# The last 16 steps of a chunked recurrence: PSUM tiles for each batch, a repeated product, and a copy placed one unit later

## The chip, the cores and the metric

The kernel runs on one core of a Trainium2 chip. The metric is the device time of one execution in microseconds (us). The program is one launch, and everything is in float32. A core has TensorE (PE, matrix products into PSUM), VectorE (DVE), ScalarE (ACT), GpSimd (POOL) and SyncE (SP), each with its own queue, and a set of DMA engines that move data between HBM and SBUF.

## The reference, cut to what matters

The input is x of shape 4 x 128 x 64 x 64: four images ("batches"), 128 channels, 4096 positions each. Layer 0 is an attention over the positions of the group-normed input, added to x. Layer 1 is a causal attention over the same 4096 positions as tokens, added, and then a recurrent block, also added:

```python
Wx = einsum('bti,hi->bth', layernorm(t), W)
Wx = (Wx - mean) * rsqrt(var + eps) * gamma + beta      # mean, var over all tokens
def step(yt, wx_t):
    yt = sigmoid(wx_t + yt @ V.T)
    return yt, yt
_, ys = scan(step, zeros, Wx over time)
t = t + ys
```

The recurrence runs along the 4096 tokens of each batch, and each step needs the step before it.

## The kernel before, in words

**The attention part** takes nearly all of the time. Its work is cut into units (`units`), in each of which a pair of key blocks of 128 is scored against a tile of up to 512 queries (`score`), exponentiated by ScalarE and multiplied with the values (`product`). Side work (normalisation, projections, the recurrence's input) is written as Python generators that are advanced one `yield` per unit by `step`. `ffn` (L745 on) makes the recurrence's input of one tile: it normalises a tile of the layer-1 output, multiplies it with W and lets ScalarE copy the product into the buffer `WX` (L772). The last query tile of the last batch is cut into two parts of 384 and 128 queries (`LAST` = 384), so that only the small part is left when the attention ends.

**The recurrence** follows. A batch's 4096 tokens are cut into chunks, of 16 tokens for batches 0 and 1 (256 chunks) and of 32 for batches 2 and 3 (128 chunks), and all chunks of a batch advance side by side as columns of one product. A chunk begins with 12 warm-up steps (`WARM`) over the last 12 tokens of the chunk before it, from a state of 0.5; a check at the end (`ok`, L1114 on) compares the state after the warm-up with the state that the chunk before it ended with, and a general kernel would run if they differed. So batches 0 and 1 have 12 + 16 = 28 steps, and batches 2 and 3 have 12 + 32 = 44. `last` is 28.

There are three chains of steps (`chains`): batch 0, batch 1, and batches 2 and 3 together. For a chain, `seed` (L1045) lets VectorE write gain times WX of two steps into a PSUM tile of one bank, `advance` (L1064, L1065) lets TensorE add FV times the state y to one step's part of the tile, and then ScalarE apply the sigmoid and write the new state into the buffer where WX of that token was. The tag of a chain (`y0`, `y1`, `y2`) has two PSUM tiles in turn. In steps 0 to 27 the three chains stand in for each other: while one waits for its sigmoid, the others compute.

From step 28 on only batches 2 and 3 are left. `advance` then splits the chain into its two batches (the list `parts`), as two products and two sigmoids in each step; both write to and read from the same PSUM tile. After each of these steps the kernel issues one product of zeros with 512 columns into a spare tile (`idle(rest, 1)`, recorded at L566, the line of the helper).

VectorE also adds the states to the residual as they get ready (`residual`, L1069), eight or four tokens of a batch at a time; the list `late` holds the additions of batches 1, 2 and 3, and a loop hands out at most one per step from step 28 on. When a batch is complete, `store` (L1074) issues two transfers of 1 MB each: batches 0 and 1 from SP's queue, batches 2 and 3 one half from SP's and one from ScalarE's queue. After the last additions VectorE works out the check (L1114 to L1123), TensorE sums it over the partitions (L1125), VectorE writes the result (L1126, L1127), and all engines load it (L1135) and branch (L1136) over the general kernel to the end of the program.

**The order of the instructions** on each engine is made when the program is built, by a scheduler that goes by the order in the source, by what depends on what and by its own estimate of when operands are ready. It also sets the semaphore waits. Where two engines touch the same PSUM tile, it orders them by the tile's bank and not by the columns that each touches. TensorE, VectorE and ScalarE each take their instructions in the order so made.

Of the kernel before, what the change touches and what calls it, by code (L numbers as in the profile page):

```python
# [25 lines left out]
F32 = mybir.dt.float32  # L26
AF = mybir.ActivationFunctionType
ALU = mybir.AluOpType
# [3 lines left out]
P = 128  # L32
QT = 512
# [432 lines left out]
WARM = 12  # L466
# [8 lines left out]
def fast_kernel(  # L475
# [9 lines left out]
    nc = tc.nc  # L485
# [4 lines left out]
    NC = [N // ch for ch in CHUNK]  # L490
# [23 lines left out]
    def load(src, shape, name):  # L514
        t = const.tile(shape, F32, name=name)
        nc.scalar.dma_start(out=t, in_=src)
        return t
# [12 lines left out]
    FV = load(fv, [P, C], "FV")  # L530
# [24 lines left out]
    WX = [wxpool.tile([P, CHUNK[b] // 2, NC[b], 2], F32, name=f"WX{b}") for b in range(2)]  # L555
    WXp = wxpool.tile([P, 2, CHUNK[2] // 2, NC[2], 2], F32, name="WXp")
# [6 lines left out]
    def idle(ps, n):  # L563

        for _ in range(n):
            nc.tensor.matmul(ps, lhsT=nil, rhs=nil.unsqueeze(1).to_broadcast([P, QT // P, P]), start=True, stop=True)  # L566
# [6 lines left out]
    with ExitStack() as actx:  # L573
# [10 lines left out]
        def misc(name):  # L584
            return ps_m.tile([P, QT], F32, tag="m", name=name)
# [107 lines left out]
        def deviations(src, eps, name):  # L693

            n = src.shape[-1] // P
            pt = misc(f"pt_{name}")
            for j in range(n):
                nc.tensor.transpose(pt[:, ts(j, P)], src[:, ts(j, P)], ident)  # L698
            stats = small.tile([P, 4, 6], F32, tag="lst", name=f"lst_{name}")
            mv = small.tile([P, 4, 2], F32, tag="lmv", name=f"lmv_{name}")  # L700
            for j in range(n):
                nc.vector.bn_stats(stats[:, j, :], pt[:, ts(j, P)])
            for j in range(n):
                nc.vector.bn_aggr(mv[:, j, :], stats[:, j, :])
            rstd = small.tile([P, 4], F32, tag="rstd", name=f"rstd_{name}")
            rsqrt(rstd[:, :n], mv[:, :n, 1], eps, n)
            return pt, mv, rstd[:, :n]

        def spread(r, name):

            n = r.shape[-1]
            g = small.tile([P, 4, 4], F32, tag="g", name=f"g_{name}")
            for q in range(4):
                nc.vector.tensor_copy(g[0:32, :n, q], r[ds(32 * q, 32), :])
            for q in range(1, 4):
                nc.vector.tensor_copy(g[ds(32 * q, 32), :n, :], g[0:32, :n, :])
            rb = tmp.tile([P, QT], F32, tag="r", name=f"rb_{name}", bufs=2)[:, : n * P]
            nc.vector.transpose(
                rb.rearrange("p (k j) -> p k j", j=32),
                g[:, :n, :].rearrange("p j q -> p (j q)").unsqueeze(2).to_broadcast([P, 4 * n, 32]),  # L720
            )
            return rb
# [23 lines left out]
        def ffn(b, c, off, w):  # L746
            name = f"f_{b}_{c}_{off}"
            cols = ds(c * QT + off, w)
            src = X2[b][:, cols]
            if b < len(kept):  # L750
                nc.sync.dma_start(out=kept[b][:, cols], in_=src)
            yield
            _, _, rstd = deviations(src, 1e-5, name)
            yield
            pw = misc(f"pw_{name}")[:, :w]
            if off == 0:
                wt[b, c] = tmp.tile([P, QT], F32, tag="w", name=f"w_{name}")
            part = wt[b, c][:, ds(off, w)]
            if w == QT - LAST:
                nc.tensor.matmul(pw, lhsT=FWc, rhs=src, start=True, stop=True)  # L760
                raw = tmp.tile([P, QT], F32, tag="a", name=f"raw_{name}")[:, :w]
                nc.scalar.copy(raw, pw)
                prow = misc(f"prow_{name}")
                idle(prow, 7)
                nc.tensor.matmul(prow[:, :w], lhsT=rstd.to_broadcast([P, P]), rhs=ident, start=True, stop=True)
                nc.vector.tensor_tensor(part, raw, prow[:, :w], ALU.mult)
                idle(misc(f"idle_{name}"), 5)
            else:
                rb = spread(rstd, name)
                nc.tensor.matmul(pw, lhsT=FWc, rhs=src, start=True, stop=True)  # L770
                nc.vector.tensor_tensor(part, pw, rb, ALU.mult)
            nc.scalar.copy(  # L772
                WX[b][:, :, ds((c * QT + off) // CHUNK[b], w // CHUNK[b]), :].rearrange("p l s t -> p s l t"),
                part.rearrange("p (s l t) -> p s l t", l=CHUNK[b] // 2, t=2),
            )
            if off + w == QT:
                nc.vector.bn_stats(stats_f[:, b * NQ + c, :], wt.pop((b, c)))
            yield
# [59 lines left out]
        for b in range(B):  # L838
            for layer in range(2):
                for c in range(NQ):  # L840
                    parts = [(0, LAST), (LAST, QT - LAST)] if (b, layer, c) == (B - 1, 1, NQ - 1) else [(0, QT)]
                    for off, w in parts:
                        n = (c * QT + off + w) // P if layer else NB
# [160 lines left out]
    with ExitStack() as fctx:  # L1004
        xback = fctx.enter_context(tc.tile_pool(name="xback", bufs=1))
        small = fctx.enter_context(tc.tile_pool(name="fsmall", bufs=1))
        ps_y = fctx.enter_context(tc.tile_pool(name="ps_y", bufs=2, space=PSUM))
# [8 lines left out]
        gain = small.tile([P, 1], F32, name="fgain")  # L1016
        rsqrt(gain, mv[:, 1:2], 1e-5, 1)
        nc.vector.tensor_tensor(gain, gain, Fgamma, ALU.mult)
        bias = small.tile([P, 1], F32, name="fbias")
# [8 lines left out]
        firstp = small.tile([P, 2, NC[2]], F32, name="firstp")  # L1028
        first = [small.tile([P, NC[b]], F32, name=f"first{b}") for b in range(2)] + [firstp[:, 0], firstp[:, 1]]
        for t in (first[0], first[1], firstp):  # L1030
            nc.gpsimd.memset(t, 0.5)
        steps = [list(range(ch - WARM, ch)) + list(range(ch)) for ch in CHUNK]
        where = {}

        def seed(g, k):

            b, m = chains[g][0], len(chains[g])
            if 2 * k >= len(steps[b]):
                return
            ps = where[g, k] = ps_y.tile([P, 2, m, NC[b]], F32, tag=f"y{g}", name=f"py{g}_{k}")  # L1040
            if k < 2:
                idle(ps.rearrange("p t h s -> p (t h s)"), 1)
            l, lo = steps[b][2 * k] // 2, int(2 * k < WARM)
            src = WXp[:, :, l] if m > 1 else WX[b][:, l].unsqueeze(1)
            nc.vector.tensor_scalar(  # L1045
                ps[:, :, :, lo:].rearrange("p t h s -> p h t s"),
                src[:, :, : NC[b] - lo, :].rearrange("p h s t -> p h t s"), gain, None, ALU.mult,
            )

        def advance(g, n):  # L1050
            b, m = chains[g][0], len(chains[g])
            if n >= len(steps[b]):
                return
            lo = int(n < WARM)
            l = steps[b][n]

            parts = [slice(h, h + 1) for h in range(2)] if n >= last else [slice(0, m)]
            for hs in parts:
                s0 = firstp[:, hs] if m > 1 else first[b].unsqueeze(1)
                wx = WXp[:, hs] if m > 1 else WX[b].unsqueeze(1)  # L1060
                dst = s0[:, :, 1:] if lo else wx[:, :, l // 2, :, l % 2]
                y = dst if lo else s0 if n == WARM else wx[:, :, (l - 1) // 2, :, (l - 1) % 2]
                ps = where[g, n // 2][:, n % 2, hs, lo:]
                nc.tensor.matmul(ps, lhsT=FV, rhs=y, start=False, stop=True, skip_group_check=True)  # L1064
                nc.scalar.activation(dst, ps, AF.Sigmoid, bias=bias)  # L1065

        def residual(b, l, n):
            xj = X[b].rearrange("p (s l t) -> p l s t", l=CHUNK[b] // 2, t=2)[:, l // 2 : (l + n) // 2]
# [2 lines left out]
        def store(b):  # L1071
            for h in range(2):
                eng = nc.scalar if h and b > 1 else nc.sync
                eng.dma_start(out=out[b, :, ts(h, N // 2)], in_=X[b][:, ts(h, N // 2)])  # L1074
# [4 lines left out]
        last = len(steps[0])  # L1079
        rest = ps_y.tile([P, QT], F32, tag="rest", name="rest", bufs=1)  # L1080
# [1 line left out]
        late += [(b, l, 8) for l in range(0, CHUNK[2] - 8, 8) for b in (2, 3)]  # L1082
        late += [(b, l, 4) for l in (CHUNK[2] - 8, CHUNK[2] - 4) for b in (2, 3)]
        for n in range(len(steps[2])):
            for g in range(3):
                advance(g, n)
            if n >= last:
                idle(rest, 1)
            if n == WARM - 1:
                for t in (first[0][:, 0:1], first[1][:, 0:1], firstp[:, :, 0:1]):  # L1090
                    nc.vector.memset(t, 0.0)
            if n % 2:
                for g in range(3):
                    seed(g, n // 2 + 2)
            if WARM < n < last and (n + 1) % 4 == 0:
                residual(0, n - WARM - 3, 4)
                if n == last - 1:
                    store(0)
            elif n >= last and late and WARM + late[0][1] + late[0][2] <= n:
                b, l, k = late.pop(0)  # L1100
                residual(b, l, k)
                if b == 1 and l + k == CHUNK[1]:
                    store(1)
# [73 lines left out]
```

## Time and profile before

| What | Value |
|---|---|
| Median of 3 runs | 2572.41 us (2571.79 to 2572.5) |
| The profiled execution: its time | 2572.15 us |
| The profiled execution: its span | 2570.4 us |
| First product of the recurrence starts | 2485.3 us |
| First product of step 28 starts | 2524.23 us |
| Last sigmoid ends | 2555.22 us |
| Last residual addition ends | 2555.93 us |
| Last stores issued (SP and ScalarE queues) | 2555.96 and 2555.97 us |
| The check's result written | 2559.91 us |
| Busy over the span: PE, DVE, ACT, POOL | 98%, 69%, 44%, 8% |
| Granted TensorE clock, mean | 0.991 |

The span is counted from the first to the last record of the profile; the execution's own time is 1.75 us longer. Times inside the execution are given from the span's start. The share of busy time is an average over stages that have different limits: the attention fills TensorE, and the last stage does not. In a line of the chain view the columns are the start in us, the length in us, and the engine, the tile written and the line; x2 is the number of records merged. One float32 product is recorded as two MATMULs.

### The profile page before, as it was taken

The page shows a single profiled execution, that of the slowest core. Times are in us where ns is not written, and L with a number is a line of the kernel's source. Part 1 is how long each engine was busy: PE and PEld are TensorE (multiplying, and loading weights), DVE is VectorE, ACT ScalarE, POOL GpSimd, SP SyncE. Part 2 cuts the span into 40 slices and gives each one's busy share as a digit, 9 for nine tenths or more (in the row PEclk, how much of TensorE's full clock was granted, in tenths as well). Part 3 has the DMA queues.
Part 4 walks back from the last instruction along what each step waited for, and adds up shares of the span by engine and source line. Part 5 has one row for each costly group of instructions (what it writes and reads, how often), then busy time and mean ns, then how long its engine had stood idle before and what let it go on. Part 6 is the DMA issues. An engine that isn't in the chain of part 4 may idle for free.

```text
span 2570.4 us, 22293 instructions
## 1 busy us (share of the span) xinstructions
PE 2514.2 (98%) x7596; PEld 1370.0 (53%) x7596; DVE 1771.7 (69%) x3534; ACT 1140.2 (44%) x1432; POOL 194.5 (8%) x281
## 2 busy tenths in 40 slices
PE   7999999999999999999999999999999999999996
PEld 4555554444555555444555555444455555544574
DVE  6776667557867677666777676765687666776565
ACT  4444434444444444444444444444444444444464
POOL 2010001101000100110100010111000000000000
PEclk9999999999999999999999999999999999999997
DMA  2000000000100000000100000000010000000013
GB/s 73 1 0 1 0 1 13 9 5 5 37 1 1 1 0 5 13 4 9 37 1 0 1 0 1 13 9 4 5 38 0 1 1 0 1 0 1 1 66 132
DMA packets 11946, 31.33 MB, mean 12 GB/s; under 512 B 2096, under 2 KB 2864, under 8 KB 10032
## 3 DMA queue, kind: packets, MB, share of 16 engines
q1 hardware_dynamic: 9216, 26.22, 2.8%
q10 hardware_dynamic: 2608, 3.61, 0.4%
q8 instruction: 61, 1.00, 0.2%
q14 instruction: 61, 0.50, 0.1%
HBM read 15.14 MB, written 14.68 MB: 12 GB/s over the span
## 4 chain that ended last, share of the span: by engine, by line
PE 90%; DVE 7%; issue 1%; ACT 1%; POOL 1%; DMA 0%; SPq 0%; POOLq 0%; DVEq 0%; ACTq 0%
PE av L966 48%; PE ps L928 17%; PE ps L921 16%; PE py L1064 2%; DVE total L963 2%; PE po L829 1%; PE pv L675 1%; PE pq L740 1%; PE pw_f L770 1%; PE pk L659 1%; PE pt L698 1%; PE pt_f L698 0%; ACT s L930 0%; POOL rstd_f L571 0%; ACT WXp L1065 0%
## 5 line engine op out<-in xcount | busy, mean ns | idle before, releaser
L963 DVE TENSOR_TENSOR total<-total,s 128x1024 f32<-128x1024 f32 (+5 forms) x810 | 881.7, 1091 | 563.1 <-ACT s L930 325.2
L966 PE MATMUL av<-s,WXp 128*128 128x512 f32 x2048 | 964.1, 593 | 0.9 <-ACT s L930 0.9
L930 ACT ACTIVATE s<-ps,shift 128x1024 f32<-128x1024 f32 x512 | 569.3, 1113 | 758.1 <-PE ps L928 737.1
L928 PE MATMUL ps<-q,K 128*128 128x512 f32 x2048 | 758.0, 492 | 2.6 <-DVE q L689 1.4
L934 ACT ACTIVATE s<-ps,zero,R 128x512 f32<-128x512 f32 (+3 forms) x607 | 404.5, 717 | 462.6 <-PE ps L921 461.1
L966 PEld LDWEIGHTS av<-s,WXp 128*128 128x128 f32 x2048 | 382.4, 189 | 299.3 <-issue 257.4
L928 PEld LDWEIGHTS ps<-q,K 128*128 128x128 f32 x2048 | 385.7, 189 | 291.6 <-issue 235.0
L966 PE MATMUL av<-s,V 128*128 128x512 f32 (+3 forms) x1214 | 505.0, 538 | 2.0 <-ACT s L934 1.7
L921 PE MATMUL ps<-q,X 128*128 128x512 f32 (+3 forms) x1214 | 503.5, 537 | 0.0
L921 PEld LDWEIGHTS ps<-q,X 128*128 128x128 f32 x1214 | 224.9, 190 | 236.3 <-issue 219.5
L966 PEld LDWEIGHTS av<-s,V 128*128 128x128 f32 x1214 | 222.0, 190 | 224.5 <-issue 195.6
L571 POOL TENSOR_TENSOR rstd<-rstd,mhalf 128x4 f32<-128x4 f32 x32 | 32.7, 1021 | 964.4 <-DVE rstd L570 964.4
L656 POOL TENSOR_SCALAR X<-X,B0v 128x512 f32<-128x512 f32 x32 | 67.5, 2112 | 250.6 <-DVE xg L654 249.1
L937 POOL TENSOR_SCALAR_AFFINE_SELECT s<-s 128x128 f32<-128x128 f32 x128 | 46.2, 366 | 519.6 <-ACT s L934 519.2
L731 DVE TENSOR_SCALAR V<-pt,lmv,rstd 128x128 f32<-128x128 f32 x128 | 43.7, 403 | 35.7 <-POOL rstd L571 35.7
L571 POOL TENSOR_TENSOR rstd_f<-rstd_f,mhalf 128x4 f32<-128x4 f32 (+2 forms) x33 | 35.8, 1085 | 408.6 <-DVE rstd_f L570 408.6
L689 DVE TENSOR_TENSOR q<-QR,qh 64x512 fp32r<-64x512 f32 x64 | 43.9, 685 | 6.3 <-PE ps L928 5.5
L671 ACT CAST K<-kh 64x512 fp32r<-64x512 f32 x32 | 19.7, 617 | 62.3 <-DVE kh L669 62.2
L797 DVE TENSOR_TENSOR t<-total 128x512 f32<-128x512 f32 x64 | 44.1, 689 | 4.4 <-PE pfw L615 2.5
L799 DVE STREAM_TRANSPOSE tt<-t 128x512 f32<-128x512 f32 x64 | 45.3, 708 | 1.9
L814 DVE SCALAR_TENSOR_TENSOR o<-rb,av 128x512 f32<-128x512 f32 x64 | 43.6, 681 | 4.1
L812 DVE STREAM_TRANSPOSE rb<-z 128x512 f32<-128x512 f32 x64 | 45.0, 703 | 1.1
(152 smaller groups left out, 1322.2 us busy)
## 6 DMA issues: line engine op xcount, KB each, us to landing
X<-in_x SPq DMA_DIRECT2D x28, 256.0 KB, 5.1
kept<-X SPq DMA_DIRECT2D x24, 256.0 KB, 2.0
Y<-kept SPq DMA_DIRECT2D x6, 1024.0 KB, 7.8
out<-Y SPq DMA_DIRECT2D x5, 1024.0 KB, 6.0
X<-in_x ACTq DMA_DIRECT2D x4, 256.0 KB, 5.4
out<-Y ACTq DMA_DIRECT2D x1, 1024.0 KB, 6.8
out<-X SPq DMA_DIRECT2D x1, 1024.0 KB, 9.7
out<-X ACTq DMA_DIRECT2D x1, 1024.0 KB, 12.6
```

The lines of the kernel that those rows point to most:

```text
L571: nc.gpsimd.tensor_tensor(dst, dst, mhalf[:, :n], ALU.pow)
L656: nc.gpsimd.tensor_scalar(xt, xt, B0v, None, ALU.add)
L799: nc.vector.transpose(tt, t)
L812: nc.vector.transpose(rb, z[:, :k].unsqueeze(2).to_broadcast([P, k, 32]))
L921: nc.tensor.matmul(ps[:, h, first[h] : w], lhsT=lhsT, rhs=q[:, off + first[h] : off + w], start=True, stop=True,)
L928: nc.tensor.matmul(ps[:, h, :], lhsT=lhsT, rhs=q[:, k, :], start=k == 0, stop=k == 1)
L930: nc.scalar.activation(s, ps, AF.Exp, bias=shift)
L934: nc.scalar.activation(part, ps[:, h, first[h] : w], AF.Exp, scale=scale, bias=zero)
L937: nc.gpsimd.affine_select(out=edge, in_=edge, pattern=[[1, P]], base=0, channel_multiplier=-1, compare_op=ALU.is_ge, fill=0.0,)
L963: nc.vector.tensor_tensor(t, t, s[:, h, f:w], ALU.add)
L966: nc.tensor.matmul(av[:, first[h] : w], lhsT=V[:, 2 * u + h, :], rhs=s[:, h, first[h] : w], start=u == 0 and h == 0, stop=2 * u + h == n - 1,)
L1064: nc.tensor.matmul(ps, lhsT=FV, rhs=y, start=False, stop=True, skip_group_check=True)
```

## The change

Three edits are made.

- In `ffn`, for the two parts of the last tile, one more `yield` stands ahead of ScalarE's copy into WX, so the copy is written one unit later in the source.
- From step 28 on, `advance_alone` takes the place of the split in `advance`. Each of batches 2 and 3 has its own PSUM tiles, made by `seed_alone`: a tile holds four steps of one batch (one bank), under the tags `y0` and `y1` that batches 0 and 1 no longer need, two tiles each in turn. The seeds for steps 28 to 31 and 32 to 35 are written at steps 25 and 27, those for 36 to 39 and 40 to 43 at steps 31 and 35.
- After each of these steps `advance_alone` issues the product of batch 3 once more (128 columns, the same state y, into the spare tile `rest`, where nobody reads it), and the product of zeros is gone.

```diff
--- before.py
+++ after.py
@@ -769,6 +769,8 @@
                 rb = spread(rstd, name)
                 nc.tensor.matmul(pw, lhsT=FWc, rhs=src, start=True, stop=True)
                 nc.vector.tensor_tensor(part, pw, rb, ALU.mult)
+            if w < QT:
+                yield
             nc.scalar.copy(
                 WX[b][:, :, ds((c * QT + off) // CHUNK[b], w // CHUNK[b]), :].rearrange("p l s t -> p s l t"),
                 part.rearrange("p (s l t) -> p s l t", l=CHUNK[b] // 2, t=2),
@@ -1035,8 +1037,6 @@
         def seed(g, k):
 
             b, m = chains[g][0], len(chains[g])
-            if 2 * k >= len(steps[b]):
-                return
             ps = where[g, k] = ps_y.tile([P, 2, m, NC[b]], F32, tag=f"y{g}", name=f"py{g}_{k}")
             if k < 2:
                 idle(ps.rearrange("p t h s -> p (t h s)"), 1)
@@ -1047,22 +1047,37 @@
                 src[:, :, : NC[b] - lo, :].rearrange("p h s t -> p h t s"), gain, None, ALU.mult,
             )
 
+        def seed_alone(h, k):
+
+            ps = where["alone", h, k] = ps_y.tile([P, 4, NC[2]], F32, tag=f"y{h}", name=f"pz{h}_{k}")
+            l = steps[2][4 * k] // 2
+            nc.vector.tensor_scalar(
+                ps.rearrange("p (l t) s -> p l t s", t=2),
+                WXp[:, h, l : l + 2].rearrange("p l s t -> p l t s"), gain, None, ALU.mult,
+            )
+
+        def move(ps, y, dst):
+            nc.tensor.matmul(ps, lhsT=FV, rhs=y, start=False, stop=True, skip_group_check=True)
+            nc.scalar.activation(dst, ps, AF.Sigmoid, bias=bias)
+
         def advance(g, n):
             b, m = chains[g][0], len(chains[g])
-            if n >= len(steps[b]):
-                return
             lo = int(n < WARM)
             l = steps[b][n]
-
-            parts = [slice(h, h + 1) for h in range(2)] if n >= last else [slice(0, m)]
-            for hs in parts:
-                s0 = firstp[:, hs] if m > 1 else first[b].unsqueeze(1)
-                wx = WXp[:, hs] if m > 1 else WX[b].unsqueeze(1)
-                dst = s0[:, :, 1:] if lo else wx[:, :, l // 2, :, l % 2]
-                y = dst if lo else s0 if n == WARM else wx[:, :, (l - 1) // 2, :, (l - 1) % 2]
-                ps = where[g, n // 2][:, n % 2, hs, lo:]
-                nc.tensor.matmul(ps, lhsT=FV, rhs=y, start=False, stop=True, skip_group_check=True)
-                nc.scalar.activation(dst, ps, AF.Sigmoid, bias=bias)
+            s0 = firstp if m > 1 else first[b].unsqueeze(1)
+            wx = WXp if m > 1 else WX[b].unsqueeze(1)
+            dst = s0[:, :, 1:] if lo else wx[:, :, l // 2, :, l % 2]
+            y = dst if lo else s0 if n == WARM else wx[:, :, (l - 1) // 2, :, (l - 1) % 2]
+            move(where[g, n // 2][:, n % 2, :, lo:], y, dst)
+
+        def advance_alone(n):
+
+            l = steps[2][n]
+            for h in range(2):
+                y = WXp[:, h, (l - 1) // 2, :, (l - 1) % 2]
+                move(where["alone", h, n // 4][:, n % 4], y, WXp[:, h, l // 2, :, l % 2])
+
+            nc.tensor.matmul(rest[:, : NC[2]], lhsT=FV, rhs=y, start=True, stop=True)
 
         def residual(b, l, n):
             xj = X[b].rearrange("p (s l t) -> p l s t", l=CHUNK[b] // 2, t=2)[:, l // 2 : (l + n) // 2]
@@ -1082,16 +1097,20 @@
         late += [(b, l, 8) for l in range(0, CHUNK[2] - 8, 8) for b in (2, 3)]
         late += [(b, l, 4) for l in (CHUNK[2] - 8, CHUNK[2] - 4) for b in (2, 3)]
         for n in range(len(steps[2])):
-            for g in range(3):
-                advance(g, n)
-            if n >= last:
-                idle(rest, 1)
+            if n < last:
+                for g in range(3):
+                    advance(g, n)
+            else:
+                advance_alone(n)
             if n == WARM - 1:
                 for t in (first[0][:, 0:1], first[1][:, 0:1], firstp[:, :, 0:1]):
                     nc.vector.memset(t, 0.0)
-            if n % 2:
+            if n % 2 and n + 3 < last:
                 for g in range(3):
                     seed(g, n // 2 + 2)
+            elif n in (last - 3, last - 1) or n >= last and n % 4 == 3 and n + 5 < len(steps[2]):
+                for h in range(2):
+                    seed_alone(h, (last // 4 if n == last - 3 else (n + 1) // 4 + 1))
             if WARM < n < last and (n + 1) % 4 == 0:
                 residual(0, n - WARM - 3, 4)
                 if n == last - 1:
```

## The prediction

> **What bounds the kernel now.** I read the page first, then the chain that ended last, then the clock by windows, then the timeline of the end.
>
> ```profile
> span 2570.4 us, 22293 instructions
> PE   7999999999999999999999999999999999999996
> PEclk9999999999999999999999999999999999999997
> ```
>
> The attention fills TensorE in every slice but the first and the last. All three edits lie in the last 100 us, so the average says nothing about them. The chain of the last 50 us shows their stage (start, length, what).
>
> ```profile
> 2528.34 0.51 PE py L1064 x2
> 2528.86 0.02 issue
> 2528.88 0.39 ACT WXp L1065
> 2529.27 0.04 issue
> 2529.31 0.51 PE py L1064 x2
> ...
> 2530.27 0.51 PE py L1064 x2
> 2530.78 0.02 issue
> 2530.81 0.64 ACT WXp L1065 x2
> 2531.45 0.04 issue
> ...
> 2540.12 0.81 PE py L1064 x2
> 2540.93 0.02 issue
> 2540.96 0.38 ACT WXp L1065
> ```
>
> To see: a product and a sigmoid take turns with no work between them, although there are two independent batches. One link is 0.51 + 0.02 + 0.39 + 0.04 = 0.96 us. Two steps are four products and four sigmoids in three links, of 0.97, 0.96 and 1.22 us (only the third, at the border of two tiles, overlaps two batches): 3.15 us, 1.57 per step. Later a product takes 0.81. The clock by windows says why (length, then busy us and records on PE, PEld, DVE, ACT, POOL; the last three columns are granted clock, DMA share and GB/s):
>
> ```profile
> 2524.23:2528.34 4.11, 3.86 (x21) 2.78 (x20) 3.78 (x5) 1.76 (x5) 0.00 (x0) 1.00 0.96 393
> 2528.34:2534.64 6.30, 3.42 (x16) 2.24 (x16) 4.90 (x6) 2.78 (x8) 0.00 (x0) 0.96 0.99 410
> 2534.64:2555.22 20.58, 13.66 (x38) 9.24 (x38) 7.92 (x12) 7.09 (x19) 0.00 (x0) 0.50 0.00 0
> ```
>
> The products of zeros were hoisted: the last runs at 2527.6. Some 6 us later the clock halves and two steps take 4.21 us. The end, from the timeline:
>
> ```profile
> 2555.24 0.69 DVE L1069 TENSOR_TENSOR X<-X,WXp 128x512 f32<-128x512 f32 x1 [0.37 <-ACT WXp L1065]
> 2555.96 0.33 SPq L1074 DMA_DIRECT2D out<-X  x1
> 2559.77 0.14 DVE L1127 CAST wrong<-good 1x1 int32<-1x1 f32 x1
> ```
>
> The last addition releases the last stores; the check ends 3.98 us after it; the span ends 14.47 us after it. In that time 4 MB go out at up to 430 GB/s until about 2566, and the slowest branch (TensorE's, issued at 2561.3) lasts 7.74 us, to 2569.05.
>
> **What the Trainium skill says.** "PSUM — Partial Sum Buffer", section "PSUM bank collisions raise a hardware error": two engines must not touch one bank in the same partitions at once, even in different columns, while different banks are free. The trace agrees with the order that follows: batch 3's product starts 0.04 us after batch 2's sigmoid has read their shared bank. "TensorE: Matmul & The Clock Gate", Part 1: the array's clock has two states, full and half, set by how busy the array was in windows of 3.41 us. The trace shows 1.00 and 0.50, and products of 0.51 and 0.81 us. "Runtime: NRT & Kernel Launch", section "Instruction fetch mechanics": a taken branch outside the loaded pages waits for a DMA fetch; the 7.74 us branch beside the stores agrees.
>
> **Part 1, the later copy: 0.** Where it stood, ScalarE waited 1.45 us for it at 2471.8, with exponentials behind, and TensorE idled 1.7 us, so a real move might gain up to about 1.5. But in the built program the order on all five queues is the same up to the recurrence, this copy's place included. Nothing moves, no DMA with it.
>
> **Part 2, own PSUM tiles.** In the built order, batch 2's product of step n+1 waits for batch 2's sigmoid of step n alone, and batch 3's likewise; from step 28 on there are no other waits than for a seed at each fourth step. At full clock, from a batch-2 product at T: its sigmoid starts at T+0.53 and ends at T+0.92; the next product starts at T+0.96. Batch 3's product follows 0.22 behind (two merged products take 0.72 where one takes 0.50), its sigmoid 0.26 behind the first (0.64 for two, 0.38 for one), both inside the 0.96. Step 28 starts at 2524.23 as before: its input is the last sigmoid of step 27. The sigmoids of step 43 end 15 x 0.966 + 0.92 + 0.26 = 15.67 us later.
>
> **Part 3, the repeated product.** It needs no new state. At 0.22 us it makes TensorE's work 3 x 0.22 = 0.66 of each 0.966 us: hidden. One exception: for step 40 the scheduler put it ahead of batch 2's product, and there it waits for batch 3's sigmoid of step 39: 0.26 + 0.22 = 0.5 us on the path. So the last sigmoid ends at 2524.23 + 15.67 + 0.5 = 2540.4, against 2555.22: 14.8 us earlier. The 16 products of zeros (0.22 each) go: those from 2522.4 to 2528 ran in the links' gaps; two ran near 2484 and 2485.7, before the recurrence's first links. Gone, they leave TensorE idle, on no path.
>
> **VectorE** is now close to the path; its order, additions at 1.17 us (2.35 for two) and seeds at 0.68: after 2520.7 two seeds, an addition, two seeds, batch 0's last addition (to 2525.7, store at 2525.8 instead of 2523.7), an addition, to 2526.9. The next seed waits for step 31's sigmoid (2528.0), with batch 1's last addition queued behind it. Seeds to 2529.4; four additions to 2534.1; seeds for step 40 to 2535.4, needed at 2536.3: 0.9 us to spare. Then three additions and two of 0.69, to 2540.3. The last two wait for step 43's sigmoids (2540.1, 2540.4) and end at 2541.5. Against 2555.93 that is 14.4 us. Stores of batches 0 and 1 (4 MB from 2525.8 and 2530.3, some 10 us at 400 GB/s) are out by about 2537, before the last four, whose two queues see the same order as before.
>
> The check: its first four subtractions now come after the last addition, about 1.2 us where 0.21 showed. It ends at 2541.5 + 1.2 + 3.77 = 2546.5, 13.4 us earlier. If the stores set the end the gain is 14.4, if the check and the branch do, 13.4; both ended within a microsecond before. I take 14.0: span 2556.4, profiled time 2572.15 - 14.0 = 2558.15. The median shown is 0.26 above that execution, so 2558.4.
>
> **Bounds of what no row shows.** Whether 0.66 of 0.966 us of products keeps the clock: before, a full clock held at 0.22 + 0.69 = 0.91 of 0.96 (one product, three of zeros), and fell after 6 us at 0.27 (four products of 0.22 in 3.15). Upper end: kept, 0 loss. Lower end: it falls 6 us in, at 2530.2, and ten steps take at least 0.81 + 0.02 + 0.38 + 0.04 = 1.26 us (three products of 0.42 fill just that): 10 x 0.3 + 0.3 for the exception = 3.3 us lost. I take kept, since real products are now spread over all steps.
>
> **The rivals.** Clock falls in the tail: 2561.7; for it, the fall before; against, more than twice the activity. VectorE is late: it carries 16.6 busy us in 31 before and almost the same work in 16 now; additions at their single price, 1.22, or a seed stuck behind them, move step 40 and the last additions by 1 to 2.5 us: about 2560. No change: the two batches still take turns, if a wait that I misread ties them, or transfers alone set the end; against it, the separate waits, and DMA idle from 2534.64 to 2554.7. Slower: the clock falls in the three-chain stage (2485 to 2522.8), because the two early products of zeros no longer bridge the wait around 2484 to 2485.7. There TensorE is the bound, so each 3.41 us window at half clock costs 1.7 us; from nine such windows (15.3 us) this outweighs the 14. Eleven cost 18.7: 2577. Against it: what is lost is 0.45 us of a window in which six zero products still run, and one chain restarts the array at 2485.3.
>
> **How the numbers follow.** Clock kept, 0.72: 2558.4, own range 2557.2 to 2559.6 (end set by stores or check, 13.4 to 14.4, and some tenths on links). Clock falls in the tail, 0.16: 2561.7. VectorE late, 0.06: 2560. No change, 0.03: 2572. Slower, 0.03: 2577. Two executions of this kernel differ by less than 0.2% (5 us), which is what a measurement can tell from no change. The first three cases all gain more, so faster 0.94, same 0.03, slower 0.03. The range 2556.8 to 2562.6 holds the first three with their edges.
>
> **What the profile after would show.** Right: links in the tail of 0.96 us with two batches in each, 31 us becoming about 16; clock 1.00 to the end of the steps; last addition near 2541.5, last stores with it; ScalarE's 1.45 us wait at 2471.8 unchanged. Wrong: products of 0.81 us before 2540; TensorE waiting for VectorE's seeds (the tile pz) at step 36 or 40; sigmoids of the two batches still alternating with products one by one; or an end that follows the last addition by more than 15 us.

## The result and the profile after

The change takes 2557.3 us (median; 2556.64 to 2559.0) against 2572.41 us: a ratio of 0.9943, with a 95% interval of 0.9929 to 0.9958. It is faster by 0.57%, and 2558.4 us was forecast. The profiled execution took 2556.64 us, its span 2554.8 us. The page of the kernel after:

```profile
span 2554.8 us, 22329 instructions
PE   7999999999999999999999999999999999999997
PEclk9999999999999999999999999999999999999997
```

As before, the averages don't show it. The chain of waits does (start, length, what):

```profile
2522.41 0.72 PE pz L1060 x4
2523.13 0.23 PE rest L1080 x2
2523.36 0.02 issue
2523.37 0.75 PE pz L1060 x4
2524.12 0.23 PE rest L1080 x2
...
2533.53 0.66 ACT WXp L1061 x2
2534.18 0.04 issue
2534.22 0.50 PE rest L1080 x2
```

Where product and sigmoid took turns, one link of 0.96 to 0.97 us now holds the products of both batches (0.72 to 0.75, four records) and the repeated one (0.23). The sigmoids run beside it and are off the chain nearly throughout. The second part of the fence is the step from 39 to 40: the sigmoids of step 39 end, and the repeated product, 0.50 us, runs ahead of step 40's own products. The clock by windows (length, busy us and records on PE, PEld, DVE, ACT, POOL; granted clock, DMA share, GB/s), with the same first two lengths as those shown of before:

```profile
2522.41:2526.52 4.11, 4.09 (x26) 3.36 (x27) 2.79 (x4) 2.54 (x8) 0.00 (x0) 1.00 0.47 191
2526.52:2532.82 6.30, 6.30 (x42) 5.26 (x41) 6.30 (x8) 4.12 (x13) 0.00 (x0) 1.00 1.02 423
2532.82:2538.53 5.71, 5.03 (x32) 3.91 (x31) 5.52 (x8) 3.61 (x12) 0.00 (x0) 1.00 0.32 131
```

The clock stays at 1.00 to the last sigmoid at 2538.53; before, it was 0.50 in the last 20.58 us of the steps. VectorE is busy nearly throughout from 2526.24 on. The timeline, with ScalarE's copy near the end of the attention ahead of the program's end:

```profile
2469.96 0.52 ACT L774 COPY WXp<-w_f 128x384 f32<-128x384 f32 x1 [1.46 <-DVE w_f L771]
...
2538.90 0.68 DVE L1084 TENSOR_TENSOR X<-X,WXp 128x512 f32<-128x512 f32 x1
2539.01 0.33 SPq L1089 DMA_DIRECT2D out<-Y  x1
2539.61 0.33 SPq L1089 DMA_DIRECT2D out<-X  x1
2544.30 0.14 DVE L1146 CAST wrong<-good 1x1 int32<-1x1 f32 x1
```

**Where the time went.** The two spans differ by 15.6 us, but 1.8 of it was already there when step 28 began (2522.41 against 2524.23), and it isn't the change's: the change's own second profile, taken later, starts step 28 at 2524.51. What the change does is measured from step 28 on. From the first product of step 28 to the end of the span there were 2570.4 - 2524.23 = 46.2 us; now there are 2554.8 - 2522.41 = 32.4 us, and in the second profile 2556.9 - 2524.51 = 32.4 us. The change is worth 13.8 us by the traces. By the medians it is 15.1 us here and 13.9 us where both kernels were measured again (2571.42 and 2557.53), so the difference is one of the spread between executions.

### The profile page after: what moved, and what is told of

It reads as the page before. It is cut to its first block, busy times and chain, and to the rows that moved or that the text cites. A ratio compares the mean times of both kernels' runs of the same rounds, so it can differ in the third digit from the quotient of the medians.

```text
span 2554.8 us, 22329 instructions
## 1 busy us (share of the span) xinstructions
PE 2506.5 (98%) x7612; PEld 1367.5 (54%) x7612; DVE 1771.1 (69%) x3534; ACT 1139.8 (45%) x1432; POOL 194.7 (8%) x281
## 4 chain that ended last, share of the span: by engine, by line
PE 88%; DVE 7%; ACT 2%; issue 1%; POOL 1%; POOLq 0%; DVEq 0%; ACTq 0%
PE av L968 48%; PE ps L930 17%; PE ps L923 16%; DVE total L965 2%; PE pv L675 1%; PE po L831 1%; PE pk L659 1%; PE pq L740 1%; PE pw_f L770 1%; PE pt L698 1%; ACT WX L1061 1%; ACT s L932 0%; POOL rstd_f L571 0%; PE pt_f L698 0%; PE pz L1060 0%
```

## The experiments

The theory was: the gain comes from the batches' own PSUM tiles, which end the turns of product and sigmoid and with them the idle time that let the clock fall; the repeated product only guards the clock, and the later copy does nothing. The rivals: the repeated product makes the gain, through the clock; ScalarE's wait for the copy could not be had anyway; and, once the first were settled, what sets the very end.

Each kernel's stage is given from its own start of step 28, since executions differ by up to 2 us before it. A ratio is to the kernel before as measured beside that run (medians 2571.09, 2571.42 and 2572.04 us), and so does not follow from the first row. All times in us:

| Kernel | Median | Ratio to before (95%) | Step 28 to last sigmoid | Step 28 to end |
|---|---|---|---|---|
| before | 2572.41 | 1 | 31.0 | 46.2 |
| the change | 2557.3 | 0.9943 (0.9929 to 0.9958) | 16.1 | 32.4 |
| the change again | 2557.53 | 0.9946 (0.9932 to 0.996) | 16.1 | 32.4 |
| tiles_none | 2556.8 | 0.9946 (0.9929 to 0.9962) | 15.65 | 32.1 |
| tiles_zeros | 2557.36 | 0.9946 (0.993 to 0.9963) | 15.65 | 31.9 |
| repeat_only | 2573.46 | 1.0007 (1.0 to 1.0013) | 33.5 | 48.6 |
| repeat_both | 2566.08 | 0.9978 (0.997 to 0.9986) | 25.8 | 40.8 |
| copy_pool | 2555.74 | 0.9941 (0.9925 to 0.9958) | as the change | 32.4 |
| check_early | 2557.76 | 0.9948 (0.9934 to 0.9962) | as the change | 32.3 |
| reduce_twice | 2556.71 | 0.9943 (0.9926 to 0.9959) | as the change | 32.0 |
| no_store3 | 2551.61 | 0.9921 (0.9904 to 0.9937) | as the change | 27.8 |
| better | 2555.16 | 0.9937 (0.9924 to 0.9951) | 15.6 | 31.7 |

### Own tiles without the repeated product, or with zeros in its place

tiles_none is the change with this edit; tiles_zeros has `idle(rest, 1)` on that line instead.

```diff
                 move(where["alone", h, n // 4][:, n % 4], y, WXp[:, h, l // 2, :, l % 2])
-            nc.tensor.matmul(rest[:, : NC[2]], lhsT=FV, rhs=y, start=True, stop=True)
```

> The change without the repeated product: nothing keeps TensorE busy in the last 16 steps but the two products of each step. Theory (the gain comes from the batches' own PSUM tiles, the repeated product only guards the clock): the links stay 0.96 us with two batches in each, and step 40's 0.5 us exception is gone. Products are then 0.44 of each 0.966 us, 46%. If that keeps the full clock, the last sigmoid ends 15.6 us after step 28 starts, and the time is about 0.5 us below that of the change (some 2556.8). If it does not, the clock falls some 6 us into these steps, about ten links take 1.26 us in place of 0.966, the sigmoids end some 18.6 us after step 28's start, and the time is some 2.5 to 3 us above that of the change (some 2560). Rival (the repeated product makes the gain, by keeping TensorE's clock full): most of the 15 us is lost again, 2567 to 2572.

> The change with the products of zeros of before in place of the repeated product. Zeros wait for nothing, and in the built order the last of them stands near step 33, so the last ten steps have none. Theory: links of 0.96 us with two batches in each throughout. If 46% of products keeps the clock, as without any filler, 2556.8; if not, the clock falls some 6 us after the last zeros, near step 39, and four or five links of 1.26 us cost 1.2 to 1.5 us: about 2558. Rival (the repeated product makes the gain): 2567 to 2572.

Both kept the clock, the lower of the theory's two values: from step 28 to the last sigmoid it takes 15.65 us in both, 15.6 expected. The windows of tiles_none and then the last one of tiles_zeros, columns as above:

```profile
2528.40:2534.70 6.30, 5.14 (x28) 3.77 (x27) 6.30 (x8) 4.19 (x13) 0.00 (x0) 1.00 1.02 421
2534.70:2539.94 5.24, 3.95 (x21) 2.96 (x20) 5.24 (x8) 3.78 (x12) 0.00 (x0) 1.00 0.35 144
```

```profile
2534.67:2539.91 5.24, 3.83 (x21) 2.84 (x20) 4.38 (x6) 3.66 (x12) 0.00 (x0) 1.00 0.35 147
```

The clock is 1.00 in all of them, and in the windows ahead of them. In tiles_none there is nothing but the two real products in each link, 0.44 of 0.966 us; in tiles_zeros the last zeros run near 2529, so its last ten steps have no more than that either. (The busy time of PE in these lines is longer than that, as ends of matmuls are modelled.) So the rival falls: the whole gain is there without the repeated product. What that product adds is step 40's half microsecond: the sigmoids end 16.1 - 15.65 = 0.5 us earlier without it, though the end comes only 0.3 us earlier, because VectorE, busy without a pause in both lines of tiles_none, then sets when the last additions are done. The own tiles also hold four steps where the shared one held two, and no run tries the one without the other; but the turns within the two steps of one shared tile, which the prediction shows, do not depend on how many steps a tile holds.

### The repeated product with the tile still shared

repeat_only is the kernel before with the zeros replaced; repeat_both has the new line one level deeper, so that it follows the product of each batch.

```diff
                 nc.scalar.activation(dst, ps, AF.Sigmoid, bias=bias)
+            if n >= last:
+                nc.tensor.matmul(rest[:, : NC[2]], lhsT=FV, rhs=y, start=True, stop=True)
...
-            if n >= last:
-                idle(rest, 1)
```

> The kernel before with the repeated product in place of the zeros, and the two batches still sharing a PSUM tile per two steps. Theory (the shared bank is the wait): product and sigmoid of the two batches go on taking turns, three links for two steps. If the clock stays full, two steps take 3.15 us, the 16 steps 25.2 us in place of 31, and the time is about 2566.5 to 2567.5. If the clock falls some 6 us in, as products are only 6 x 0.22 of 3.15 us (42%), it is about that of before, 2572 to 2575. Rival (the repeated product makes the gain): 2558, the time of the change.

> The kernel before, its shared PSUM tile included, with a repeated product behind each of the two products of a step in place of the zeros: eight products of 0.22 us in 3.15 us, 56%. It separates what the shared tile costs by its wait from what it costs by letting the clock fall. Theory (both, the wait more): the clock stays full and the turns stay, three links in 3.15 us for two steps; the last sigmoid ends about 25.3 us after step 28 starts, in place of 31, and the time is about 2566, where one of the twenty executions with a single repeated product already lay. If the clock still falls: 2572 to 2575. Rival (only the clock matters, the wait is nothing): 2556 to 2558.

The windows of repeat_only and then of repeat_both, at the same places:

```profile
2523.69:2527.80 4.11, 3.10 (x14) 2.22 (x14) 2.42 (x3) 1.51 (x5) 0.00 (x0) 0.87 0.92 375
2527.80:2534.10 6.30, 5.24 (x17) 4.07 (x18) 4.89 (x5) 2.27 (x6) 0.00 (x0) 0.50 1.00 416
```

```profile
2523.69:2527.80 4.11, 3.60 (x22) 2.82 (x23) 2.64 (x4) 1.76 (x5) 0.00 (x0) 1.00 0.95 387
2527.80:2534.10 6.30, 5.31 (x34) 4.13 (x34) 4.90 (x6) 2.77 (x8) 0.00 (x0) 1.00 0.99 410
```

With one repeated product the clock has fallen before 2528, earlier than with the zeros, and stays at half: the kernel is as slow as before (2573.46 us, where 2572 to 2575 was expected for a fallen clock). With two it stays full, and the chain of waits of repeat_both shows the turns still there:

```profile
2534.62 0.39 ACT WXp L1065
2535.01 0.04 issue
2535.05 0.51 PE py L1064 x2
```

That is the chain's old form at full clock: the lone product that starts at 2535.05 comes again at 2538.21, two steps or 3.16 us later. The theory's 2566 was met (2566.08), and so was the 25.3 us, nearly (25.8). The two costs of the shared tile can now be told apart. From step 28 to the end: 46.2 to 40.8, so 5.4 us were the clock; 40.8 to 32.1 (tiles_none), so 8.7 us were the turns themselves; 0.3 are given back by the repeated product at step 40. Together 13.8. Measured to the last sigmoid the turns are 10.2 us; 1.5 of them do not reach the end, which VectorE's additions and the stores set. The split takes the repeated products of repeat_both to cost nothing, and is good to some half microsecond.

### The copy moved in earnest

```diff
-            if w < QT:
-                yield
-            nc.scalar.copy(
+            eng = nc.gpsimd.tensor_copy if w == LAST else nc.scalar.copy
+            eng(
```

> The change with the 384-wide copy of the last quarter tiles moved from ScalarE to GpSimd, in place of the later place in the source, which moved nothing in the built order. Theory (a copy that really leaves ScalarE's queue takes away its 1.46 us wait near 2470, and TensorE's idle time of 1.7 to 1.9 us with it): TensorE's idle time there falls below 0.5 us, and the time is 1 to 1.5 us below that of the change. Rival (that wait is covered, TensorE then waits for the next thing as long): no difference to the change.

The timeline of copy_pool at the place:

```profile
2470.82 0.64 POOL L773 COPY WXp<-w_f 128x384 f32<-128x384 f32 x1 [3.06 <-DVE w_f L771]
2471.18 0.81 ACT L935 ACTIVATE s<-ps,zero,R 128x128 f32<-128x128 f32 x2 [0.58 <-PE av L967]
2471.69 0.49 PE L967 MATMUL av<-s,V 128*128 128x128 f32 x2 [0.55 <-ACT s L935]
```

ScalarE no longer stands behind VectorE's `w_f`, and the last idle time of TensorE there is 0.55 us in place of 1.72. From the same six exponentials (at 2462.55 in the change, 2463.37 here) to the product `pz` after the attention (2473.54, 2472.92) it takes 9.55 us in place of 10.99, which is 1.44 us less, and from there to the end both need 81.3 us. So the wait that the later copy left in place was worth 1.4 us, as the theory had it (the idle time left, 0.55 us, is just above the 0.5 that it gave as the most). The ratios can't show so little; beside tiles_none and tiles_zeros, which ran with it, the median is 1.1 and 1.6 us lower.

### What sets the end

The prediction left open whether the stores or the check with the branch behind it end the program. check_early issues the comparisons of batches 0 and 1 at steps 28 and 29 (the place of the call is shown; they no longer stand after the last addition), reduce_twice repeats the check's reduction, and no_store3 leaves out batch 3's two stores, so that a quarter of the output is not written:

```diff
+            if n in (28, 29):
+                compare(n - 28)
```

```diff
         nc.vector.tensor_reduce(good[:, 0:1], ok, AX.X, ALU.min)
+        nc.vector.tensor_reduce(good[:, 0:1], ok, AX.X, ALU.min)
```

```diff
-            if l + k == CHUNK[b]:
+            if l + k == CHUNK[b] and b != 3:
                 store(b)
```

> The change with the comparisons of the check for batches 0 and 1 issued early in the last 16 steps, in place of after the last addition, where the profile shows 0.75 us for them. Theory (the check and the slow branch behind it set the end, which in all kernels so far lies 10.3 to 10.5 us after the check's last operation): the check ends 0.7 us earlier after the last addition, the span ends 10.4 us after the check again, and the time is 0.5 to 0.75 us below that of the change. Rival (the last stores set the end): the span still ends 15.2 us after the last stores are issued, and the time is that of the change.

> The change without batch 3's stores, so that half of the last 4 MB and a quarter of the output are never written. Theory (the end is set by when the last four stores have drained, 13.4 to 14.0 us after the first of them is issued, and the span ends 1.8 us later in every kernel): 2 MB less is some 5 us less of transfers at 400 GB/s, the branch's 6.9 us wait beside them shortens too, and the time is 2 to 5 us below that of the change, 2553 to 2555.5. Rival (the check and a branch of a length of its own set the end, and the stores only fit beside it): the span still ends 10.3 to 10.5 us after the check's last operation, and the time is that of the change, 2557.5.

> The change with the check's reduction, 0.95 us, done twice, so that the check ends about 1 us later while the stores are issued as before. Theory (the stores' drain sets the end): the wait at the branch is about 6 us in place of 6.9, the span ends 1.8 us after the last landing as before, and the time is that of the change, 2557.5. Rival (check and branch set the end): the wait stays 6.9 us, the span ends 10.4 us after the check, and the time is 1 us above that of the change, 2558.5.

My theory ahead of check_early was that the check sets the end; it fell. The check ended 0.7 us earlier against the last addition, and nothing was gained. SyncE's wait at the branch (the view of waits: us in total, times, longest) in the change, in check_early and in reduce_twice:

```profile
SPq L1155 <- SPq L1155: 7.0, 2, 6.9
```

```profile
SPq L1161 <- SPq L1161: 7.7, 2, 7.5
```

```profile
SPq L1156 <- SPq L1156: 4.4, 2, 4.2
```

A check that ends earlier waits longer at the branch, and one that ends 1 us later waits less (4.2 us, and then 1.1 for TensorE's branch): 10.4 us from the check's last operation to the end became 11.0 and 9.0. TensorE's branch, the slowest, took 7.56 us in the change, 7.80 in check_early, 6.65 in reduce_twice, and 4.06 in no_store3. So the branch has no length of its own here. What holds it is the drain of the stores: in the eleven profiles of kernels that issue all four of the last stores, the end comes 15.2 to 15.8 us after the first of them, and 9.0 to 11.1 us after the check. Windows of the kernel before, of the change, and then of no_store3:

```profile
2554.70:2565.65 10.95, 0.69 (x3) 0.50 (x2) 4.00 (x9) 0.37 (x1) 0.00 (x0) 0.50 0.93 382
2565.65:2570.40 4.75, 0.00 (x0) 0.00 (x0) 0.00 (x0) 0.00 (x0) 0.00 (x0) 0.50 0.07 19
```

```profile
2539.00:2550.00 11.00, 0.59 (x2) 0.50 (x2) 4.58 (x11) 0.00 (x0) 0.00 (x0) 0.66 0.93 381
2550.00:2554.80 4.80, 0.00 (x0) 0.00 (x0) 0.00 (x0) 0.00 (x0) 0.00 (x0) 0.50 0.07 19
```

```profile
2539.73:2545.40 5.67, 0.59 (x2) 0.50 (x2) 4.57 (x11) 0.00 (x0) 0.00 (x0) 0.78 0.89 368
2545.40:2550.90 5.50, 0.00 (x0) 0.00 (x0) 0.00 (x0) 0.00 (x0) 0.00 (x0) 0.50 0.07 16
```

The last four stores, 4 x 1.05 MB, go out at 381 GB/s in 11.0 us from the first of them (382 GB/s and 10.95 us before), and some 4.8 us later, with only small transfers in between, the program ends. With half the bytes the stage is 32.4 - 27.8 = 4.6 us shorter by the trace (by the medians 5.7 and 5.9 below the change, and 5.1 below reduce_twice, which ran beside it; I had given 5 as the most). There the drain and the check end within 0.3 us of each other (2545.4 and 2545.15), so this run doesn't say which of the two the last 5.5 us wait for; in the change it is the drain. That the small transfers of the last 5 us are the instructions behind the branch fits what the Trainium skill says ("Runtime: NRT & Kernel Launch", section "Instruction fetch mechanics"), but no run here tells whose they are.

### The pieces together

better is the change without the repeated product, with the copy on GpSimd, and with the comparisons and squares of batches 0 and 1 on GpSimd at step 28 (of the edit, only this last part is shown).

```diff
+            if n == 28:
+                compare(0)
+                compare(1)
+                nc.gpsimd.tensor_tensor(two, two, two, ALU.mult)
```

> The change without the repeated product, with the last copy on GpSimd, and with the comparisons and squares of batches 0 and 1 done early on GpSimd. Theory: the gains add: 0.5 us (no repeated product ahead of step 40), 1.4 us (ScalarE's wait gone), and on the check 0.75 for the comparisons and 0.5 for the shorter square, of which the stores may hide a part. Sum 1.9 to 3.1 us below the change: about 2554 to 2555. Rival: GpSimd's work beside VectorE's additions lengthens them and the last addition comes later by as much: no difference to the change.

> The change itself, beside the others. All theories: 0.9943 of the time before; its profile shows whether the clock's dip near 1881 us, which its first profile lacks and all the others have, comes back. If the dip is chance, the step-28 start moves by some 1.8 us with it and the length of the last 16 steps stays 16.1 us.

better took 2555.16 us (2554.34 to 2555.55), the change beside it 2557.53 us (2556.06 to 2558.81): 2.4 us less, and no execution of the one reaches into the range of the other. The trace accounts for 2.1 of it: 1.4 from the copy and 32.4 - 31.7 = 0.7 from step 28 on. The measured 2.4 lies in the 1.9 to 3.1 that was expected. As check_early gained nothing, the check's share of that is hidden by the stores; what the 0.7 has beyond the repeated product's 0.3 to 0.5 is no more than this stage differs by among the change, check_early and reduce_twice (32.0 to 32.4). VectorE's additions are 1.22 us beside GpSimd's work as without it, so the rival falls too.

## Why the prediction was right, point by point

- **Part 1, the copy, 0: right.** ScalarE waits 1.46 us for `w_f` at 2469.96 as it waited 1.45 before. That a real move would be worth "up to about 1.5" was right too (1.44, copy_pool).
- **Part 2, the link: right.** 0.96 to 0.97 us with both batches in it, 15.65 us from step 28 to the last sigmoid without the exception, where 15.67 was worked out.
- **Part 3, the repeated product: right on all counts.** No wait of its own, hidden in the link, and the exception at step 40 costs 0.5 us: 16.12 us with it, 16.17 predicted. Corrected for the 1.82 us that the execution was early, the last sigmoid ends 14.9 us earlier, where 14.8 was forecast.
- **The clock kept: right, and with room.** I gave 0.16 to a fall at 66% of products; even at 46% it stayed (tiles_none). So the chance of a fall was set too high for this kernel, though not out of place: with a shared tile, at 42% on the average, the clock fell (repeat_only).
- **VectorE: right in size.** The seeds for step 40 are done at 2533.5 and used at 2534.5, 1.0 us to spare where 0.9 was worked out. The last addition ends 14.5 us earlier (corrected), 14.4 forecast. Of the rival "VectorE is late" a trace is left: without step 40's exception VectorE sets the end of the additions.
- **The end, 13.4 to 14.4, taken 14.0: right by luck of the middle.** The step named the right two candidates, but sized the stores' one wrongly. I counted it from the last addition, which was forecast 14.4 us earlier and came 14.5 earlier. What counts is the first of the four last stores, since all four go out at one rate from its issue on: 2554.70 before, 2539.01 now, corrected 13.9 earlier, with 15.7 us from there to the end before and 15.8 now. That gives the 13.8. The last two pairs of stores had been 1.26 us apart and are 0.60 now, so the second pair's lead was lost in the queue. The check's 13.4 was right by itself (13.6) but bounds nothing. One of the prediction's own signs of being wrong did come, by a little: the end follows the last addition by 15.2 us (14.5 before), and more than 15 was to be such a sign.
- **No change and slower:** neither came. The clock in the three-chain stage stayed 1.00 without the two early products of zeros.

The forecast of 2558.4 is 1.1 us above the median, and with the end's term put right it would be 1.3 above. That is in size what executions differ by before step 28, where the change does nothing.

## What to carry to other kernels

Two independent chains that share a PSUM tile are, as this kernel is scheduled, not independent: look in the chain of waits for a product and a sigmoid that take turns one by one, and give each chain its own tile. Here such turns were paid twice, once as waiting (8.7 us) and once as a lower clock (5.4 us), so cost a change in them at full clock and at half, and test a filler and the wait apart before one is given the credit. Where a program ends in stores as this one does, count from the first store of the last batch of them and not from the last, and try a later check before working on an earlier one.

## What was unexpected of the hardware

- **How little keeps the clock.** Products at 0.44 of each 0.966 us (46%) kept it full for the whole stage. At six of 0.22 in 3.15 us (42% on the average) it fell in the profiled execution of repeat_only at 2526.7, 3 us into the stage, and in the 3.4 us ahead of that the share was lower: five products or a little more, about a third. One of the twenty executions of repeat_only took 2566.26 us with a mean clock of 0.996, which is what repeat_both takes with 56%; the other nineteen took 2571.04 to 2574.82. So in this kernel chance decides, and no run here says at which share, or over what length of time, the clock falls. The Trainium skill ("TensorE: Matmul & The Clock Gate", Part 1) names an idle window as what lowers the clock, and in one of its examples frequent short idle times. The trace fits the second: in repeat_only no idle time of TensorE in the steps around the fall was over 0.6 us, so the clock fell without a long one.
- **Short dips in the attention that come by chance.** Around 655, 1270 and 1885 us the mean clock of a 10 us window falls to as little as 0.83 in some executions and not in others of the same kernel: the change's first profile has one of these dips, its second all three, before all three. In the kernel before, the first and the third are 3.4 us each at half clock (653.4 to 656.8 and 1882.2 to 1885.6). The profiles of before and of the change with three start step 28 at 2524.2 and 2524.5, those of the change and of reduce_twice with one at 2522.4 and 2522.2; five others with two dips start it at 2523.1 to 2524.3. At some 1 us each they fit most of the spread between executions, and they are why a difference of 1 us has to be read from a stage of the trace. At each of the three places TensorE has just stood idle for 2.2 us, in executions with the dip and in those without (at 653 us 2.25 in the change's second profile, with it, and 2.23 in copy_pool, without). What starts one and not the other was not tried.
